# A row pool of its own, down weights behind the rows, and a later last routing in a two-layer mixture-of-experts kernel

## The chip, the cores and the metric

The kernel runs as one program on one core of a Trainium2 chip. The metric is the device time of one execution in microseconds (us). TensorE (PE) does the matrix products and the transposes, VectorE (DVE) and ScalarE (ACT) the elementwise work and the copies out of PSUM, GpSimd (POOL) issues the indirect DMAs (scatters and gathers by a list of row numbers), and SyncE (SP) issues most of the plain DMAs. An engine takes its instructions in order. A DMA issue that has to wait on a semaphore holds back everything queued behind it on the engine that issues it.

## The reference

Eight sequences of 512 tokens with 256 features, in float32, go through two pre-norm layers:

```python
x = x + L0_attn(layernorm(x))   # causal, 16 query heads, 4 key/value heads, rotary
x = x + L0_ffn(layernorm(x))    # 32 experts of inner size 96, top 8 of a softmax, weights renormalized
x = x + L1_attn(layernorm(x))   # causal, 16 heads, biases
x = x + L1_ffn(layernorm(x))    # 16 experts of inner size 176, top 2, and one shared expert of 352
# an expert e: (silu(t @ gate_e) * (t @ up_e)) @ down_e, times the token's routing weight
```

Layernorm is over the features and has no scale or bias.

## The kernel before

**Stages.** The first attention runs sequence by sequence in a software pipeline; after each sequence comes its routing (`routed0`): normalize, turn, router scores, top 8, and then 32 indirect DMAs on POOL (line 427, `xg<-xn_f,rows_f`) that scatter the token rows into a table `xg` in DRAM, ordered by expert. The experts of layer 0 follow, then the second attention with its routing (8 scatters a sequence) and the shared expert, and then the experts of layer 1. The tokens are split into two parts (sequences 0 to 3 and 4 to 7), each with its own tables.

**Experts.** `experts` runs over pairs of tiles of 128 rows: 150 pairs in layer 0 (75 a part), some 44 in layer 1. Step `s` of the loop issues five stages, each for another pair: `load` of pair s (two DMAs from `xg` on SP, line 1141, into a tile `xg_m`, seven of them in rotation), `turn_x` of pair s-4 (PE transposes to `xgT_m`, a DVE copy to `xgTs_m`), `gate_up` of pair s-5 (products `gu_m`, silu on ACT, scaling on DVE to `h_m`), `turn_h` of pair s-6 (`hT_m`, copied to `hTs_m`) and `down` of pair s-7 (products `y_m` with the weights `dw`, line 1214, copied by ACT to `ys_m` and stored). PE's order is that of the loop, written by hand; the other engines are ordered by a scheduler. Row numbers are read into SP registers every eight tiles (line 1119).

After step 3, `load_down` issues the DMAs of the down weights on SP (line 1303): 6 of them, 3.15 MB, in layer 0; 26, 2.88 MB, in layer 1. The list `Beside` steps other work along with the pairs. In layer 0 that is the routing of the last sequence (13 steps over pairs 7 to 20), then the tables and zero rows of the second part (line 1076, `xg<-zeros`), loads of weights, and the gathers `x_a<-yg` that add the experts' results to the first sequences.

**Memory.** Pools are opened one after another and take addresses in that order; a stage's pools reuse the addresses of the stage before. A tile that lies where an older one lay waits for the last reader of the older one. In the kernel before, `xg_m` belongs to the experts' pool `moe` and lies at its bottom, below `xgTs_m`, `h_m`, `hTs_m` and `ys_m`. In the attention, `oT_a` (the turned output, read by the output products `y_a`, line 769) and `xn_f` (the normalized rows that the scatters read) are tiles that matter below.

**Normalization.** `layernorm_steps` computes statistics (lines 315, 316), the inverse root in small steps (281 to 290) and the scaled rows `xn` (325). Its argument `behind` names an instruction after which each operation is put on its engine's queue. `layernorm` runs all of it at once. For the first sequence of the second attention that instruction is the last `hTs_m` copy of the experts, so the whole normalization comes after it; later sequences use the attention's last mask product.

**Startup.** `fast0` loads the attention's weights. The key and value weights pass through one buffer `kv_in`, and the cosine and sine tables through one buffer `turnf`, so the second of each is issued on ACT's queue when the first has been read.

Of the kernel before, what the change touches and what calls it, by code (L numbers as in the profile page):

```python
# [17 lines left out]
P = 128  # L18
# [4 lines left out]
NG = 4  # L23
# [68 lines left out]
def two_blocks_kernel(  # L92
# [212 lines left out]
    def layernorm_steps(x, lnp, name, tag="xn", bufs=1, spare=0, behind=lambda: None):  # L305


        def later():
            return tc.issue_after(behind()) if behind() else ExitStack()

        stats = lnp.tile([P, NT, 6], F32, tag="stats", name=f"stats_{name}")
        mv = lnp.tile([P, NT, 2], F32, tag="mv", name=f"mv_{name}")
        for t in range(NT):
            with later():
                nc.vector.bn_stats(out=stats[:, t, :], in_=x[:, t, :])
            nc.vector.bn_aggr(out=mv[:, t, :], in_=stats[:, t, :])  # L316
            if t % 2:
                yield
        with later():
            rstd = inverse_root(mv[:, :, 1], lnp, name)  # L320
        yield
        xn = lnp.tile([P, NT, D + spare], F32, tag=tag, name=f"xn_{name}", bufs=bufs)
        for t in range(NT):
            with later():
                nc.vector.tensor_scalar(
                    xn[:, t, :D], x[:, t, :], mv[:, t, 0:1], rstd[:, t : t + 1], ALU.subtract, ALU.mult
                )
            if t % 2:
                yield
        return xn  # L330
# [501 lines left out]
    def fast0(awp, lnp, atp, late, ptp, ps, bank):  # L832
# [10 lines left out]
                nc.vector.tensor_copy(q_out[:, :, :, s, :], q_in[:, k, :, s, :, :DH])  # L843
        for n, which in enumerate("kv"):
            lo, hi = A0[which]
            kv_in = awp.tile([P, ND, NG, 32], F32, tag="kv_in", name=f"{which}_in", bufs=1)
            nc.scalar.dma_start(out=kv_in.rearrange("p k g r -> p (k g r)"), in_=a0[:, lo:hi])
            at = D + n * HKV * DH
            nc.vector.tensor_copy(
                wq[:, :, at : at + HKV * DH].rearrange("p k (g d) -> p k g d", g=HKV), kv_in[:, :, :, :DH]  # L850
            )
# [2 lines left out]
        turn = []  # L854
        for which in ("cos", "sin"):
            lo, hi = A0[which]
            f = awp.tile([DH, T], F32, tag="turnf", name=f"{which}f", bufs=1)
            nc.scalar.dma_start(out=f, in_=a0[:DH, lo:hi])
            tr = bank(f"{which}t")[:, : NT * DH].rearrange("p (t d) -> p t d", t=NT)
            for t in range(NT):  # L860
                nc.tensor.transpose(tr[:, t, :], f[:, t * P : (t + 1) * P], ident[:DH, :DH])
            w = awp.tile([P, NT, DH], F32, tag=which, name=f"{which}0")
            nc.vector.tensor_copy(w, tr)
            turn.append(w)
# [98 lines left out]

        return w, loads

    def fast1(w, v1s, lnp, atp, late, ptp, ps, bank, last):
        wv, wo, vb, ob, qkb = (w[n] for n in ("v", "o", "vb", "ob", "qkb"))
        att = Attention(1, late, ptp, ps, bank, wo, last)

        def before(b):  # L970
            x, name = xs[b], f"a1_{b}"
            xn = layernorm(x, lnp, name, behind=att.masked)
            yield from free()
            xn = yield from turned(xn, lnp, bank, name)

            nc.vector.tensor_tensor(
                x, x, ob.rearrange("p m d -> p (m d)").unsqueeze(1).to_broadcast([P, NT, D]), ALU.add
            )
            v1 = v1s[b % 2]
            for h in range(NT // 2):  # L980
                v = bank(f"v_{name}_{h}").rearrange("p (t d) -> p t d", t=2)
                for i in range(2):
                    t = 2 * h + i
                    for k in range(ND):
                        nc.tensor.matmul(
                            v[:, i, :], xn[:, k, t * P : (t + 1) * P], wv[:, k, :], start=(k == 0), stop=(k == ND - 1)
                        )
                for i in range(2):
                    nc.vector.tensor_tensor(
                        v_heads(v1, 2 * h + i, H), v[:, i, :].rearrange("p (h d) -> p h d", d=DH), vb, ALU.add  # L990
                    )
                yield
            qT = atp.tile([P, 2, T], F32, tag="qT", name=f"qT_{name}")
            kT = atp.tile([P, 2, 2, T], F32, tag="kT", name=f"kT_{name}")
            for m in range(2):
                q = bank(f"q_{name}_{m}")
                for k in range(ND):
                    nc.tensor.matmul(q, w["q"][:, k, m, :], xn[:, k, :], start=(k == 0), stop=(k == ND - 1))  # L998
                nc.vector.tensor_scalar(qT[:, m, :], q, qkb[:, 0, m : m + 1], None, ALU.add)
                yield  # L1000
                kk = bank(f"k_{name}_{m}")
                for k in range(ND):
                    nc.tensor.matmul(kk, w["k"][:, k, m, :], xn[:, k, :], start=(k == 0), stop=(k == ND - 1))
                nc.scalar.activation(
                    kT[:, m, 0, :], kk, AF.Identity, bias=kb[:, m, 0:1], scale=half[:, 0:1]
                )
                nc.vector.tensor_scalar(
                    kT[:, m, 1, :], kk, half[:, 1:2], kb[:, m, 1:2], ALU.mult, ALU.add
                )
                yield  # L1010
            att.heads[b] = lambda c: (qT[:, c // 2, :], kT[:, c // 2, c % 2, :], v1, c * NG * (DH + 1))

        return att, before
# [67 lines left out]
    class Beside:  # L1081


        def __init__(self, *items):
            self.items = []
            for item in items:
                self.add(*item)
            self.load = None
            self.last = None

        def add(self, first, last, steps, work):
            self.items.append([first, last, steps, iter(work), 0])
# [10 lines left out]
            for item in self.items:  # L1103
                drain(item[3])

    def experts(n, gu, dn, mp, ps, again, beside, load_last):

        name = f"m{n}{'g' * again}"
        jobs = [(lay, i) for lay in lays[n] for i in range(0, lay.tiles(again), 2)]
# [25 lines left out]
        def load(lay, i):  # L1135
            part = lay.part
            if i % RB == 0:
                registers(lay, i)
            xg = mp.tile([P, 2, lay.width], F32, tag="xg", name=f"xg_{name}_{part}_{i}", bufs=7)
            for j in range(2):  # L1140
                beside.load = nc.sync.dma_start(out=xg[:, j, :], in_=lay.xg[bass.ds(rows[part, i + j], P), :]).ins
            made["xg", part, i] = xg
# [53 lines left out]
        def turn_h(lay, i):  # L1196
            part = lay.part
            h = made.pop(("h", part, i))
            hp = ps.tile([P, n_ch, 2, P], F32, tag="hT", name=f"hT_{name}_{part}_{i}")
            hT = mp.tile([P, n_ch, 2, P], F32, tag="hTs", name=f"hTs_{name}_{part}_{i}")  # L1200
            for q, (lo, n_in) in enumerate(chunks):
                for j in range(2):
                    nc.tensor.transpose(hp[:n_in, q, j, :], h[:, j, lo : lo + n_in], ident)  # L1203
            beside.last = nc.vector.tensor_copy(hT[: chunks[0][1]], hp[: chunks[0][1]]).ins  # L1204
            made["hT", part, i] = hT

        def down(lay, i):
# [78 lines left out]
                in_ = src[n][:, : 2 * ND * P].rearrange("p (g c i) -> p g c i", c=ND, g=2)  # L1286
                nc.sync.dma_start(out=out_[:, g, :, at : at + hi - lo], in_=in_[:, g, :, lo:hi])

    def load_down(w, src, inner, routed):

        chunks = -(-inner // P)
        width = inner // chunks
# [5 lines left out]
        for n, lo, hi, e, at in pieces(inner, whole):  # L1298
            while lo < hi:
                q, r = at // width, at % width  # L1300
                rows = min(hi - lo, width - r)
                to = (e * chunks + q) * D
                nc.sync.dma_start(out=w[r : r + rows, :, to : to + D], in_=src[n, lo : lo + rows, :, 2 * ND * P :])
                lo, at = lo + rows, at + rows

    def read_x(b, tmp, tiles=NT):
# [92 lines left out]
    def all_experts(n, gw, gat, again=False, weights=()):  # L1399
# [6 lines left out]
        with ExitStack() as s:  # L1406
            dwp = s.enter_context(tc.tile_pool(name=f"down{n}{g}", bufs=1, reuse_waits="tile"))
            mp = s.enter_context(tc.tile_pool(name=f"moe{n}{g}", bufs=3, reuse_waits="tile"))
            small = s.enter_context(tc.tile_pool(name=f"tables{n}{g}", bufs=1, reuse_waits="tile"))
            ps = s.enter_context(tc.tile_pool(name=f"ps_m{n}{g}", bufs=2, space=PSUM, reuse_waits="tile"))  # L1410
            inner, chunks, src, routed = (I0, 1, f0, N0) if n == 0 else (I1, ND1, f1, N1R)
# [28 lines left out]
            if n == 0 and not again:  # L1440
                beside.add(8, 9, 1, x_kept())
                lnp = s.enter_context(tc.tile_pool(name="ln_last", bufs=1, reuse_waits="tile"))
                beside.add(7, 20, 13, routed0(NB - 1, lnp, bank, ffn_parts(lnp, bank)[0], lambda: beside.last))
                begin = 22
            beside.add(
                begin, min(32 + begin, first - 4), 6 + lays[n][1].n_e // 8, tables(lays[n][1], small, bank, again, beside)
            )
# [5 lines left out]
            else:  # L1453
                beside.add(
                    done, end, SPLIT[1] * 7, results(range(SPLIT[1]), gat, gat, ps, g, lambda: beside.last)
                )
            experts(n, gw, dw, mp, ps, again, beside, lambda: load_down(dw, src, inner, routed))
            return beside.last

    def routed0(b, lnp, bank, route, behind=None):  # L1460
        name = f"f0_{b}"
# [32 lines left out]
    with ExitStack() as s1:  # L1494
        wp1 = s1.enter_context(tc.tile_pool(name="attn_w1", bufs=1, reuse_waits="tile"))
        gat = s1.enter_context(tc.tile_pool(name="gather", bufs=1, reuse_waits="tile"))
        w1, loads1 = weights1(wp1)
        last = all_experts(0, gw0, gat, weights=loads1)
        with ExitStack() as s:
            awp, lnp, atp, late, ptp, smp, ps = pools(s, 1, False)  # L1500
            v1s = v_tiles(awp, 2, H, nc.vector)
            bank = banks(ps, 3)
            att, before = fast1(w1, v1s, lnp, atp, late, ptp, ps, bank, last)
            route, shared = ffn_parts(smp, bank)
            gw1 = gpool.tile([P, E1 * GU1], F32, tag="gu", name="gw1")

# [280 lines left out]
```

## Time and profile before

| what | value |
|---|---|
| median of 14 runs | 1957.71 us (1945.08 to 1967.18) |
| profiled execution, whole | 1952.44 us |
| its span, first to last instruction | 1950.6 us |
| mean granted PE clock | 0.897 |
| PE busy | 1592.0 us, 82% |
| DVE, ACT, POOL busy | 994.1, 650.4, 811.2 us |
| first attention | to about 640 us |
| experts of layer 0 | about 640 to 1132 us |
| second attention | about 1132 to 1690 us |
| experts of layer 1 and results | about 1690 to 1950 us |

The table is one profiled execution; the other runs have a time only. Busy time overlaps between engines. "Granted clock" is the share of full speed that PE was given.

### The profile page before, as it was taken

The numbers are of one execution on the slowest core, as the hardware profiler recorded it, in microseconds if no ns is written. First come the engines' busy times: TensorE is split into PE (matmuls) and PEld (weight loads), VectorE is DVE, ScalarE is ACT, GpSimd is POOL, SyncE is SP. The second block draws the span as 40 slices with busy tenths as digits, with TensorE's granted clock in tenths as the row PEclk, the third lists the DMA queues.
The fourth block names the chain that finished last, engine by engine and source line by source line (L and its number), as shares of the span: only waits on it lengthen the run. The fifth ranks groups of instructions, "written<-read, shape, count | busy, mean of one in ns | idle before, by whom it ended". The sixth has DMA issues, their size and how long they took to land.

```text
span 1950.6 us, 31020 instructions
## 1 busy us (share of the span) xinstructions
PE 1592.0 (82%) x10180; PEld 1050.0 (54%) x10180; DVE 994.1 (51%) x3179; ACT 650.4 (33%) x865; POOL 811.2 (42%) x686
## 2 busy tenths in 40 slices
PE   5977385575835658999999979999999997999995
PEld 3433142232413657989988844445444544677764
DVE  5655273453623434545555666566546645444453
ACT  3533142232412112323333334454444543222222
POOL 0041623515245151000788888388884011133332
PEclk9977696777867778999999989999999998999997
DMA  2132332522124655787999975256642022435364
GB/s 64 32 104 71 108 88 92 167 86 85 59 84 136 191 173 156 217 258 205 250 262 272 276 142 71 63 97 128 133 72 66 21 84 69 139 102 161 92 215 153
DMA packets 245721, 255.75 MB, mean 131 GB/s; under 512 B 79881, under 2 KB 224911, under 8 KB 245554
## 3 DMA queue, kind: packets, MB, share of 16 engines
q1 hardware_dynamic: 188754, 164.15, 28.1%
q0 software_dynamic: 56448, 89.18, 19.9%
q8 instruction: 88, 1.44, 0.3%
q14 instruction: 79, 0.65, 0.1%
q10 hardware_dynamic: 352, 0.33, 0.1%
HBM read 132.37 MB, written 124.32 MB: 132 GB/s over the span
## 4 chain that ended last, share of the span: by engine, by line
PE 62%; another core or an unknown queue 14%; DVE 9%; issue 6%; ACT 5%; DMA 2%; SPq 1%; POOL 0%; DVEq 0%; POOLq 0%; ACTq 0%
PE gu_m L1183 13%; PE y_m L1214 8%; PE st_a L680 8%; PE o_a L703 6%; PE xgT_m L1150 4%; ACT p_a L685 3%; PE hT_m L1203 2%; PE y_a L769 2%; PE sy_f L457 2%; PE qkv_a L887 2%; PE sg_f L444 2%; PE su_f L444 2%; DVE p_a L691 2%; PE q_a L998 1%
## 5 line engine op out<-in xcount | busy, mean ns | idle before, releaser
L427 POOL DMA_INDIRECT xg<-xn_f,rows_f x320 | 316.5, 989 | 674.3 <-DVE rec_a L719 243.5
L1263 POOL DMA_INDIRECT x_a<-yg,yrows x256 | 402.7, 1573 | 289.1 <-DVE yrows L1260 193.1
L685 ACT ACTIVATE p_a<-st_a 128x2048 f32<-128x2048 f32 (+1 forms) x192 | 306.1, 1594 | 372.9 <-PE st_a L680 230.9
L1183 PE MATMUL gu_m<-gw,xgTs_m 128*128 x1552 | 341.7, 364 | 21.1 <-issue 12.5
L680 PE MATMUL st_a<-qT_a,kT_a 32*128 32x512 f32 (+3 forms) x2048 | 217.3, 499 | 94.9 <-ACT p_a L685 76.7
L1183 PEld LDWEIGHTS gu_m<-gw,xgTs_m 128*128 128x128 f32 x1552 | 262.8, 195 | 51.5 <-issue 14.4
L691 DVE TENSOR_TENSOR p_a<-p_a,causal 128x512 f32<-128x512 f32 x256 | 170.6, 685 | 140.9 <-ACT p_a L685 127.5
L1214 PE MATMUL y_m<-dw,hTs_m 96*128 (+1 forms) x952 | 240.1, 382 | 2.7 <-DVE mv_f L316 2.7
L703 PE MATMUL o_a<-p_a,v 128*32 128x512 f32 (+3 forms) x2048 | 212.3, 476 | 19.7 <-issue 13.4
L680 PEld LDWEIGHTS st_a<-qT_a,kT_a 32*128 32x128 f32 x2048 | 96.3, 196 | 195.1 <-ACT p_a L685 103.7
L1152 DVE COPY xgTs_m<-xgT_m 128x512 f32<-128x512 f32 x194 | 133.5, 688 | 107.1 <-PE xgT_m L1150 68.5
L1219 ACT COPY ys_m<-y_m 128x512 f32<-128x512 f32 x194 | 113.7, 586 | 205.1 <-PE y_m L1214 161.3
L1214 PEld LDWEIGHTS y_m<-dw,hTs_m 96*128 96x128 f32 (+1 forms) x952 | 166.8, 192 | 18.5 <-DVE mv_f L316 2.9
L1175 DVE SCALAR_TENSOR_TENSOR h_m<-h_m,xg_m,gu_m 128x96 f32<-128x96 f32 (+1 forms) x388 | 114.7, 326 | 91.2 <-ACT h_m L1188 39.2
L1225 POOL DMA_INDIRECT yg<-ys_m,to_m x88 | 88.9, 1010 | 154.1 <-ACT ys_m L1219 139.5
L1204 DVE COPY hTs_m<-hT_m 96x256 f32<-96x256 f32 (+1 forms) x194 | 92.8, 478 | 113.9 <-PE hT_m L1203 85.0
L1150 PE MATMUL xgT_m<-ident,xg_m 128*128 128x128 f32 x776 | 121.3, 278 | 30.1 <-DMA xg_m<-xg 15.5
L1191 ACT ACTIVATE h_m<-gu_m 128x192 f32<-128x192 f32 x150 | 49.7, 331 | 253.1 <-PE gu_m L1183 183.8
L1150 PEld LDWEIGHTS xgT_m<-ident,xg_m 128*128 128x128 f32 x776 | 96.6, 143 | 54.7 <-issue 19.7
L709 DVE COPY osb_a<-o_a 128x512 f32<-128x512 f32 x64 | 44.1, 689 | 160.1 <-remote 86.8
L703 PEld LDWEIGHTS o_a<-p_a,v 128*32 128x32 f32 x2048 | 52.1, 113 | 131.7 <-issue 91.0
L1203 PE MATMUL hT_m<-ident,h_m 128*96 128x128 f32 (+1 forms) x476 | 86.1, 277 | 15.3 <-DVE h_m L1175 15.1
(206 smaller groups left out, 1704.2 us busy)
## 6 DMA issues: line engine op xcount, KB each, us to landing
xg_m<-xg SPq DMA_DIRECT2D x388, 144.0 KB
yg<-ys_m SPq DMA_DIRECT2D x150, 256.0 KB
xg<-zeros SPq DMA_DIRECT2D x100, 144.0 KB
g<-yg SPq DMA_DIRECT2D x16, 512.0 KB
xg<-xn_f,rows_f POOLq DMA_INDIRECT x320
x_after<-x_in SPq DMA_DIRECT2D x8, 512.0 KB
x_a<-x_after SPq DMA_DIRECT2D x8, 512.0 KB
x_a<-yg,yrows POOLq DMA_INDIRECT x256
```

The source lines that it names most:

```text
L427: inst = nc.gpsimd.indirect_dma_start(out=lay.xg, out_offset=bass.IndirectOffsetOnAxis(ap=rows[:, t, i : i + 1], axis=0), in_=xn[:, t, :], ...
L680: nc.tensor.matmul(st[:, g, at : at + T - j * P], kT[r, j * P : (j + 1) * P], qT[r, j * P :], start=True, stop=True,)
L685: nc.scalar.activation(pt, st[:, :, :width], AF.Exp, scale=SCALE)
L691: self.masked = nc.vector.tensor_tensor(d, d, causal.unsqueeze(1).to_broadcast([P, NG, P]), ALU.mult).ins
L703: nc.tensor.matmul(o[32 * g : 32 * g + 32, j * P :], v1[:, j, v_at + g * (DH + 1) :][:, :32], probs[n][:, g, at : at + T - j * P], start=( ...
L1150: nc.tensor.transpose(tr[:, j, c, :], xg[:, j, c * P : (c + 1) * P], ident)
L1152: nc.vector.tensor_copy(xT, tr)
L1175: nc.vector.scalar_tensor_tensor(h[:, j, :], h[:, j, :], xg[:, j, D:][:, bass.ds(offs[part, i + j][2], 1)], gus[j][:, inner:], ALU.mult, A ...
L1183: nc.tensor.matmul(gus[j], xT[:, j, c, :], gu[:, bass.ds(at + c * 2 * inner, 2 * inner)], start=(c == 0), stop=(c == ND - 1),)
L1203: nc.tensor.transpose(hp[:n_in, q, j, :], h[:, j, lo : lo + n_in], ident)
L1214: nc.tensor.matmul(y[:, j, :], hT[:n_in, q, j, :], dn[:n_in, bass.ds(at + q * D, D)], start=(q == 0), stop=(q == n_ch - 1),)
L1263: nc.gpsimd.indirect_dma_start(out=xs[b][:, t, :], out_offset=None, in_=lay.yg[: lay.tiles(bool(again)) * P, :], in_offset=bass.IndirectOf ...
```

## The change

1. The row tiles `xg_m` get a pool of their own, `rows`, opened after `moe`, so they lie above the experts' other buffers (in layer 0 at 181,696 bytes of each partition instead of 161,984; in layer 1 at 208,832 instead of 175,552).
2. `load_down` puts its DMAs behind the last row load issued so far (`beside.load`), which is the eighth.
3. The last sequence's routing steps along pairs 20 to 33 instead of 7 to 20, and the second part's tables begin at pair 36 instead of 22.
4. The first normalization of the second attention is spread: its nine groups go behind the last six `hTs_m` copies, the list of which `experts` now keeps, instead of behind the last one.
5. `kv_in` and `turnf` have two buffers each, which moves later attention tiles up by 3,072 bytes.
6. `later` calls `behind` once for each operation instead of twice, as an iterator now needs.

```diff
         def later():
-            return tc.issue_after(behind()) if behind() else ExitStack()
+            inst = behind()
+            return tc.issue_after(inst) if inst else ExitStack()
...
-            kv_in = awp.tile([P, ND, NG, 32], F32, tag="kv_in", name=f"{which}_in", bufs=1)
+            kv_in = awp.tile([P, ND, NG, 32], F32, tag="kv_in", name=f"{which}_in", bufs=2)
...
-            f = awp.tile([DH, T], F32, tag="turnf", name=f"{which}f", bufs=1)
+            f = awp.tile([DH, T], F32, tag="turnf", name=f"{which}f", bufs=2)
...
-    def fast1(w, v1s, lnp, atp, late, ptp, ps, bank, last):
+    def fast1(w, v1s, lnp, atp, late, ptp, ps, bank, copies):
-        att = Attention(1, late, ptp, ps, bank, wo, last)
+        att = Attention(1, late, ptp, ps, bank, wo, copies[-1])
...
-            xn = layernorm(x, lnp, name, behind=att.masked)
+            if b == 0:
+
+                behind = iter([copy for copy in copies[-6:] for _ in range(2)])
+                xn = whole(layernorm_steps(x, lnp, name, behind=lambda: next(behind)))
+            else:
+                xn = layernorm(x, lnp, name, behind=att.masked)
...
-            xg = mp.tile([P, 2, lay.width], F32, tag="xg", name=f"xg_{name}_{part}_{i}", bufs=7)
+            xg = xgp.tile([P, 2, lay.width], F32, tag="xg", name=f"xg_{name}_{part}_{i}")
...
             beside.last = nc.vector.tensor_copy(hT[: chunks[0][1]], hp[: chunks[0][1]]).ins
+            beside.copies.append(beside.last)
...
-    def load_down(w, src, inner, routed):
+    def load_down(w, src, inner, routed, behind):
...
-                nc.sync.dma_start(out=w[r : r + rows, :, to : to + D], in_=src[n, lo : lo + rows, :, 2 * ND * P :])
+                with tc.issue_after(behind):
+                    nc.sync.dma_start(out=w[r : r + rows, :, to : to + D], in_=src[n, lo : lo + rows, :, 2 * ND * P :])
...
             mp = s.enter_context(tc.tile_pool(name=f"moe{n}{g}", bufs=3, reuse_waits="tile"))
+
+            xgp = s.enter_context(tc.tile_pool(name=f"rows{n}{g}", bufs=7, reuse_waits="tile"))
...
-                beside.add(7, 20, 13, routed0(NB - 1, lnp, bank, ffn_parts(lnp, bank)[0], lambda: beside.last))
-                begin = 22
+                beside.add(20, 33, 13, routed0(NB - 1, lnp, bank, ffn_parts(lnp, bank)[0], lambda: beside.last))
+                begin = 36
...
-            experts(n, gw, dw, mp, ps, again, beside, lambda: load_down(dw, src, inner, routed))
-            return beside.last
+            experts(n, gw, dw, mp, xgp, ps, again, beside, lambda: load_down(dw, src, inner, routed, beside.load))
+            return beside.copies
```

More of the change, by code (lines that the diff above doesn't have):

```diff
@@ L1089, in __init__ @@
             self.last = None
+            self.copies = []
         def add(self, first, last, steps, work):
@@ L1104, in finish, with experts @@
                 drain(item[3])
-    def experts(n, gu, dn, mp, ps, again, beside, load_last):
+    def experts(n, gu, dn, mp, xgp, ps, again, beside, load_last):
         name = f"m{n}{'g' * again}"
@@ L1497, in two_blocks_kernel @@
         w1, loads1 = weights1(wp1)
-        last = all_experts(0, gw0, gat, weights=loads1)
+        copies = all_experts(0, gw0, gat, weights=loads1)
         with ExitStack() as s:
@@ L1502, in two_blocks_kernel @@
             bank = banks(ps, 3)
-            att, before = fast1(w1, v1s, lnp, atp, late, ptp, ps, bank, last)
+            att, before = fast1(w1, v1s, lnp, atp, late, ptp, ps, bank, copies)
             route, shared = ffn_parts(smp, bank)
```

## The prediction

> **What bounds it now.** I read the page first, then the chain of waits stage by stage, then the SP queue's own timeline and waits, because most of the change moves DMA issues.
>
> ```profile
> PE 62%; another core or an unknown queue 14%; DVE 9%; issue 6%; ACT 5%; DMA 2%; SPq 1%; POOL 0%; DVEq 0%; POOLq 0%; ACTq 0%
> ```
>
> The chain that ended last lies on TensorE for 62%, so an edit counts where it opens or closes a PE gap. The stretches around the edits (columns: length, busy us of PE, PE weight loads, DVE, ACT, POOL, granted clock, DMA share, GB/s):
>
> ```profile
> 641.00:658.00 17.00, 9.91 (x43) 8.74 (x44) 5.73 (x16) 0.99 (x3) 0.05 (x1) 0.68 0.74 181
> 649.00:653.00 4.00, 4.00 (x20) 3.87 (x20) 1.23 (x4) 0.66 (x2) 0.00 (x0) 0.62 1.06 236
> 658.00:698.00 40.00, 39.13 (x250) 35.94 (x249) 25.50 (x100) 14.75 (x29) 0.13 (x1) 0.96 0.65 196
> 698.00:745.00 47.00, 16.70 (x73) 13.86 (x72) 6.17 (x17) 3.46 (x8) 30.68 (x32) 0.59 0.42 145
> 1645.00:1662.00 17.00, 15.66 (x47) 10.04 (x48) 9.71 (x35) 3.65 (x5) 0.31 (x1) 0.80 0.79 180
> 1701.00:1760.00 59.00, 59.00 (x290) 44.78 (x289) 28.04 (x83) 14.12 (x35) 22.53 (x23) 1.00 0.35 108
> ```
>
> Seen here: once the first down product of a layer has run (658 and 1701), PE has no gap, so a late start is never made up. While the 32 scatters of the last sequence's routing leave POOL (698 to 745), PE works 16.7 of 47 us. The SP queue at both starts of experts:
>
> ```profile
> 606.35 2.45 SPq L1303 DMA_DIRECT2D dw<-in_f_dram  x4
> 610.16 37.18 SPq L1141 DMA_DIRECT2D xg_m<-xg  x8
> 647.38 0.93 SPq L1303 DMA_DIRECT2D dw<-in_f_dram  x2
> ...
> 1645.59 13.34 SPq L1303 DMA_DIRECT2D dw<-in_f_dram  x26
> 1660.05 9.54 SPq L1141 DMA_DIRECT2D xg_m<-xg  x14
> ```
>
> ```profile
> SPq L1141 <- remote: 28.2, 1, 28.2
> ```
>
> In layer 0 four of six down-weight loads leave at 606, under the attention's tail; then two row loads; then the third waits 28.2 us (612.05 to 640.24), until the attention's last output product. In layer 1 all 26 weight loads leave at 1645, 55 us before they are needed. The first down products, by the chain:
>
> ```profile
> 656.57 0.92 issue
> 657.49 1.12 PE y_m L1214 x4
> ...
> 1700.87 1.73 PE y_m L1214 x8
> ```
>
> In layer 0 it starts as the last weight load lands (last semaphore step at 657.4); in layer 1 nothing holds it.
>
> **Part 1: weights behind rows, layer 0: +7 us.** The new row pool lies above the expert buffers, and the two doubled startup buffers push the attention's late tiles up by 3 KB per partition. By the addresses of the built program the first row buffer now overlaps oT of the last sequence; before, the third load's buffer did. So the 28.2 us wait moves from the third load to the first, and all six weight loads stand behind eight row loads, where before four stood ahead of them. First row load at 640.35. The trace has six row loads from there to 647.38 (slow at first, 0.52 us each at the end); two more end at 648.4. Then 6 weight loads of 3.15 MB, where before 2.1 MB of it was in by 617. Rates of the nearest rows: 236 GB/s (649 to 653, mostly these weights) and 181 (641 to 658). From 649.3 that is 13.4 to 17.4 us, landing at 662.7 to 666.7 against 657.4: +5.2 to +9.2. I take +7, nearer neither end. Rows 9 and up are behind the weights and come with them. The first transposes slip some 2 us, hidden under that wait. The cover is gone from here on: PE is full after 658.
>
> The Trainium skill, "DMA: Bandwidth & Descriptors", in its anatomy of one DMA, fits a transfer as 2.0 us plus bytes over 436 GB/s. By that the 3.15 MB would take 9.2 us and this part would cost about +1; for the 2.88 MB of layer 1 it gives 8.6 us and about 0 there. No stretch of several us in which these weights move, in 1 KB packets, is above 240 GB/s, so the rows decide and the sum leaves the fit out.
>
> **Part 2: the same in layer 1: +9.5 us.** Here the first row buffer is free early, but by the built program the second pair's overlaps xn of the last sequence's routing, so the third row load waits for all eight of its scatters. The last one on POOL:
>
> ```profile
> 1685.31 0.96 POOL L427 DMA_INDIRECT xg<-xn_f,rows_f  x1 [0.30 <-issue]
> ```
>
> Its packets end at 1687.9 in the trace. SP goes on at 1688; six row loads at 0.52 us; weights from 1691.1, 26 loads. Before, these took 16.6 us from first issue (1645.6) to last packet (1662.2): so 1707.7, and 0 to 3 us more for the 0.9 MB of rows ahead. At 236 GB/s it would be 1704.5. Taken: 1708.5 against 1700.87, +7.6 (bounds +3.6 to +9.8). The first down product waits for all 26 by its semaphores. The pair's own rows (issued 1688) are in by about 1691, when needed. PE then idles some 7.6 us from a clock of 1.00. After an idle of 9 us it restarted thus:
>
> ```profile
> 743.96 0.67 PE L1203 MATMUL hT_m<-ident,h_m 128*96 128x128 f32 x2 [9.01 <-DVE h_m L1175]
> 744.42 1.92 PE L1214 MATMUL y_m<-dw,hTs_m 96*128 x4
> ```
>
> The same groups take 0.38 and 1.03 us when warm; with the next two (1.06 for 0.60, 1.77 for 1.47) that is 1.9 us lost. +1.9 (0 to 1.9); in layer 0 the trace of before already holds such a restart, so nothing is added there. PE is full to 1860, so all of it reaches the end.
>
> **Part 3: last routing at pairs 20 to 33: 0.** Same 13 steps, same 32 scatters, same table loads, 13 pairs (37 us at 2.83 us a pair) later. The stall of some 30 us in 698 to 745 moves with the scatters. Bounds from the other bursts: over eight stretches of 40 to 42 us PE was busy 13.3 to 19.8 us, so idle 22 to 28 against 30: -8 to +3. The part tables and 33 zero writes move from the loads of pairs 44 to 53 to those of 58 to 67; the rows that need them are first read at pair 75. In 825 to 845, where most of these writes leave, PE lost 2.3 us; that moves too.
>
> **Part 4: first normalization in steps: -2.7.**
>
> ```profile
> 1130.68 1.92 PE L1214 MATMUL y_m<-dw,hTs_m 96*128 x8
> 1135.92 1.69 PE L343 MATMUL xT_a<-ident,xn_a 128*128 128x128 f32 x8 [3.32 <-DVE xn_a L325]
> ```
>
> PE waits 3.32 us for the statistics. In steps they run behind the last six hT copies: 5.4 us of DVE work (4 statistics, 4 aggregates, 12 small operations, 4 scalings) in pairs where DVE has 1.65 us of work in 2.83, so 7.1 us are free. Small delays of the copies give back about 0.6. Bounds -3.3 to +1.
>
> **Part 5: startup: -0.7.**
>
> ```profile
> 4.37 4.66 DMA sinf<-in_a_dram
> ...
> 9.72 0.23 DVE sin L863
> ```
>
> The sine table was issued only when the cosine buffer was free; now at about 2.1. On DVE the query weights' copies end at 9.04, the sine's starts at 9.72: 0.7 us, then bound by the query weights' landing (about 8), a little later as the value weights now go ahead. Bounds -1.4 to 0.
>
> **Sum.** 7 + 9.5 + 0 - 2.7 - 0.7 = +13.1. The profiled execution took 1952.44 us (span 1950.6, 1.8 around it): 1965.5. It ran 5.3 below the median, 1957.71, so the forecast is 1970.8.
>
> **Rivals.** (a) *The loads come faster than the rows say*: both weight loads at 236 GB/s or better, no restart loss. Then +5.2 and +3.6 against -3.4 of gains: +5, and with row waits that end earlier about +2: 1960. For it: the layer 1 loads may have been slowed by the attention around them. Against: both stretches show DMA engines busy at 0.74 or more. 0.14.
> (b) *Faster*: the routing's burst at its new place stops PE less. The eight scatters of 1676 to 1686 left PE busy 13.6 of 14 us, so a burst needn't stop it. If two thirds or more of the 30 us go, the sum falls to -7 or below, 1951 or less; it decides from 19 us saved. Against: all eight bursts of 32 stopped PE alike, in attention and in the experts, and nothing in it is changed but its place. 0.11.
> (c) *Both starts dearer*: stragglers and rows behind the weights cost 4 to 5 us more each: 1980 and above. 0.08.
> (d) *The edit doesn't do what it says*, rows earlier: that is in the forecast, since the addresses undo it in both layers.
> Forecast: 0.67.
>
> **Numbers.** A measurement of this kernel can tell about 0.3%, 5.9 us. The forecast's own terms span +5 to +23; its lower edge touches "same". Slower 0.74, same 0.15, faster 0.11. The range leaves out most of (b) and half of (c): 1956 to 1982.
>
> **What would show it.** After: SP's wait of some 28 us ahead of the first row load at 640, six weight loads at about 648, first down product of layer 0 near 664; SP waiting until 1688 (shifted by the sum so far), the first down product of layer 1 7 to 8 us later than its transposes allow; the 3.32 us before xT_a gone. Wrong if either first down product isn't late, or if PE is busy over 30 us in the 47 us of the moved burst.

## The result and the profile after

The changed kernel takes 1977.96 us (median of 10 runs, 1969.69 to 1987.27), against 1959.4 us for the kernel before (47 runs): ratio 1.0099, 95% interval [1.0071, 1.0128], so 14 to 25 us slower. The forecast was 1970.8 us, with a range of 1956 to 1982. Its profiled execution took 1971.17 us (span 1969.5), 18.7 more than the one of before.

From the page, the shares of the chain that ended last; TensorE still carries it:

```profile
PE 61%; another core or an unknown queue 15%; DVE 8%; issue 5%; ACT 4%; DMA 3%; SPq 2%; POOL 1%; ACTq 0%; DVEq 0%; POOLq 0%
```

The SP queue at the start of layer 0 (start, length, line, operation, count), then its wait in 600 to 760:

```profile
619.51 22.72 SPq L1148 DMA_DIRECT2D xg_m<-xg  x8
642.33 3.64 SPq L1312 DMA_DIRECT2D dw<-in_f_dram  x6
646.77 14.71 SPq L1148 DMA_DIRECT2D xg_m<-xg  x9
```

```profile
SPq L1148 <- remote: 27.8, 1, 27.8
```

The wait that stood ahead of the third row load is now ahead of the first, and all six weight loads stand behind eight row loads. Before, four had left at 606. One detail is new: the wait ended at 619.37, not at 640, and then each of the eight loads took 2.8 us to issue. The same stretch by windows (length, busy us of PE, PE weight loads, DVE, ACT, POOL, granted clock, DMA share, GB/s), with the moved burst of 32 scatters in the last line:

```profile
641.00:664.00 23.00, 10.48 (x37) 9.22 (x38) 4.58 (x12) 2.86 (x5) 0.00 (x0) 0.58 0.90 207
664.00:704.00 40.00, 40.00 (x257) 37.31 (x255) 22.85 (x63) 12.82 (x28) 0.00 (x0) 1.00 0.69 210
...
736.00:783.00 47.00, 16.45 (x79) 13.04 (x77) 6.66 (x21) 3.71 (x9) 30.66 (x32) 0.75 0.44 149
```

Transfers fill the wait (DMA share 0.90), PE is then full, and the burst stops PE as before (16.45 of 47 us busy, against 16.70). The chain at the first down product of layer 0:

```profile
652.37 7.69 DMA xg_m<-xg
660.06 2.03 PE y_m L1222 x4
```

It names a row load, the last transfer to step a semaphore. By the program `y_m` reads `dw`, whose loads left SP just before on the same queue, so the weights are what it waits for; the profile alone doesn't say so. Layer 1, by the chain, the SP queue and PE's timeline:

```profile
1696.10 0.96 POOL xg L428
...
1697.36 2.43 DMA xg<-xn_f,rows_f
...
1699.99 0.33 SPq L1148
```

```profile
1676.75 26.17 SPq L1148 DMA_DIRECT2D xg_m<-xg  x8
1703.04 13.17 SPq L1312 DMA_DIRECT2D dw<-in_f_dram  x26
```

```profile
1706.44 5.06 PE L1190 MATMUL gu_m<-gw,xgTs_m 128*128 x8 [2.69 <-DVE xgTs_m L1159]
...
1720.81 2.57 PE L1222 MATMUL y_m<-dw,hTs_m 88*128 x8 [2.62 <-DMA xg_m<-xg]
```

The first line is the last scatter but one; the last starts at 1697.36 and its transfer ends at 1699.79. Then comes the third row load, then the 26 weight loads, then the first down product: each step waits for the one above it. After its wait the first group of `gu_m` takes 5.06 us where the same group later takes 2.53. At the turn to the second attention the gap of 3.32 us is gone:

```profile
1136.46 1.93 PE L1222 MATMUL y_m<-dw,hTs_m 96*128 x8
1138.22 1.04 PE L344 MATMUL xT_a<-ident,xn_a 128*128 128x128 f32 x8
```

### The stages of all runs

Lengths in us, worked out from starts and ends in the traces. *L0 start*: from the first scatter of the last burst in the first attention to the first down product. *L0 pairs*: from there to the start of the last one of layer 0. *Norm*: from there to the first `v_a`. *Attention 2*: to the last shared-expert product `sy_f`. *L1 start*: to the start of the 17th down product instruction of layer 1 (the first of its third pair), so the slow products after an idle PE are in it.

| profile | L0 start | L0 pairs | norm | attention 2 | L1 start | span |
|---|---|---|---|---|---|---|
| before | 56.9 | 474.7 | 5.9 | 551.4 | 21.2 | 1950.6 |
| after | 63.5 | 478.0 | 1.6 | 562.0 | 31.0 | 1969.5 |
| weights_first | 55.7 | 480.4 | 1.6 | 547.2 | 26.6 | 1947.3 |
| routing_back | 64.0 | 474.4 | 1.6 | 565.4 | 31.2 | 1978.0 |
| norm_startup | 54.4 | 475.4 | 1.6 | 572.0 | 21.2 | 1960.2 |
| pool_order | 54.5 | 473.0 | 8.6 | 566.5 | 32.6 | 1971.5 |
| *second chip:* before_again | 23.6 | 444.6 | 6.4 | 529.0 | 21.2 | 1659.3 |
| after_again | 28.0 | 443.9 | 1.6 | 528.4 | 31.0 | 1665.3 |
| routing_only | 20.3 | 438.4 | 6.1 | 531.4 | 21.2 | 1652.8 |
| spread_last | 23.8 | 437.8 | 1.6 | 529.5 | 21.2 | 1646.5 |
| *third chip:* after_more | 60.8 | 476.8 | 1.6 | 550.2 | 32.9 | 1957.3 |
| norm_startup_2 | 53.7 | 474.0 | 1.6 | 552.4 | 21.2 | 1938.3 |
| best_later | 53.6 | 475.4 | 1.6 | 565.6 | 21.2 | 1949.3 |
| spread_again | 51.4 | 455.3 | 1.6 | 550.5 | 21.2 | 1912.5 |

From before to after: startup -1.75 (first scatter at 113.59 against 115.34), first attention -2.2, L0 start +6.5, L0 pairs +3.2, norm -4.3, attention 2 +10.6, L1 start +9.8, the rest of layer 1 -3.0. That adds up to the +18.9 of the spans. All but attention 2 and two small negatives (first attention, rest of layer 1) belong to an edit: -1.75 + 6.5 + 3.2 - 4.3 + 9.8 = +13.5.

### The profile page after: what moved, and what is told of

It reads as the page before. It is cut to its first block, busy times and chain, and to the rows that moved or that the text cites. A ratio compares the mean times of both kernels' runs of the same rounds, so it can differ in the third digit from the quotient of the medians.

```text
span 1969.5 us, 31022 instructions
## 1 busy us (share of the span) xinstructions
PE 1589.9 (81%) x10180; PEld 1048.7 (53%) x10180; DVE 993.7 (50%) x3179; ACT 649.7 (33%) x865; POOL 808.3 (41%) x686
## 4 chain that ended last, share of the span: by engine, by line
PE 61%; another core or an unknown queue 15%; DVE 8%; issue 5%; ACT 4%; DMA 3%; SPq 2%; POOL 1%; ACTq 0%; DVEq 0%; POOLq 0%
PE gu_m L1190 13%; PE y_m L1222 8%; PE st_a L681 7%; PE o_a L704 6%; PE xgT_m L1157 4%; ACT p_a L686 3%; PE y_a L770 2%; PE hT_m L1210 2%; PE sg_f L445 2%; PE qkv_a L888 2%; PE su_f L445 2%; PE sy_f L458 2%; SPq L1148 2%; DMA xg_m<-xg 2%
## 5 line engine op out<-in xcount | busy, mean ns | idle before, releaser
L1190 PE MATMUL gu_m<-gw,xgTs_m 128*128 x1552 | 344.5, 366 | 29.6 <-DVE xgTs_m L1159 23.8
L704 PE MATMUL o_a<-p_a,v 128*32 128x512 f32 (+3 forms) x2048 | 210.8, 472 | 23.8 <-issue 17.8
L770 PE MATMUL y_a<-wo,oT_a 128*128 128x256 f32 x256 | 74.2, 436 | 28.3 <-issue 19.6
```

Source lines behind the costliest of these rows:

```text
L704: nc.tensor.matmul(o[32 * g : 32 * g + 32, j * P :], v1[:, j, v_at + g * (DH + 1) :][:, :32], probs[n][:, g, at : at + T - j * P], start=( ...
L770: nc.tensor.matmul(y[:, i, :], oT[:, k, t * P : (t + 1) * P], self.wo[:, k, :], start=(k == 0), stop=(k == ND - 1),)
L1190: nc.tensor.matmul(gus[j], xT[:, j, c, :], gu[:, bass.ds(at + c * 2 * inner, 2 * inner)], start=(c == 0), stop=(c == ND - 1),)
```

## Experiments

The theory: the two late expert starts (rows above other buffers, weights behind rows) make the kernel slower, and normalization and startup give a little back. Rivals: the second attention is itself made longer; the place of the last routing matters.

**Weights ahead of the rows again** (the change with item 2 undone):

```diff
-                with tc.issue_after(behind):
-                    nc.sync.dma_start(out=w[r : r + rows, ...
+                nc.sync.dma_start(out=w[r : r + rows, ...
```

> The changed kernel with the down weights no longer put behind the row loads (item 2 undone, the row pool stays on top). Theory (the order costs): in layer 0 four weight loads leave ahead of the blocked row loads again, so the first down product comes some 5 us earlier than in the changed kernel, and in layer 1 all 26 leave about 45 us ahead of the last scatters, so the first down product is at most 2 us late against about 10. In all some 14 us less than the changed kernel, so about 5 us over the kernel before. Rival (the row pool's addresses cost, whatever the order): the row loads still wait for the last output product and for the last scatters, the starts stay late, and the time stays within 4 us of the changed kernel's.

Measured: 1965.51 us (12 runs) against 1962.51 for before (30 runs), ratio 1.0024 [0.9995, 1.0054]. So item 2 carries most of the loss: 12 us by the medians, 15 by the two ratios. Layer 0 starts 1.3 us earlier than before. In layer 1 the expectation missed: the start is still 5.4 us late. SP there, by its timeline:

```profile
1639.52 12.97 SPq L1311 DMA_DIRECT2D dw<-in_f_dram  x26
1658.09 30.47 SPq L1148 DMA_DIRECT2D xg_m<-xg  x14
```

The weights leave early, yet the rows from the third on still wait for the scatters that read `xn_f`, whose place the row buffer overlaps: the last scatter starts at 1678.81, and the third row load leaves at 1681.44. So of the 9.8 us in layer 1 the rows alone make 5.4, and the weights behind them the rest.

**The last routing back at pairs 7 to 20** (the change with item 3 undone):

```diff
-                beside.add(20, 33, 13, routed0(NB - 1, ...
-                begin = 36
+                beside.add(7, 20, 13, routed0(NB - 1, ...
+                begin = 22
```

> The changed kernel with the last routing back at pairs 7 to 20 and the tables from pair 22 (item 3 undone). Theory (the zero rows collide with the turn from part one to part two): the stretch around pairs 67 to 80, where PE loses about 11 us to late rows in the changed kernel, loses about 3 us at pairs 50 to 58 instead, so 7 us less than the changed kernel. Rival (as predicted: the move is worth nothing): within 2 us of the changed kernel in that stretch, both terms only shifted.

Measured: 1975.56 us (7 runs), ratio 1.0074 [1.0043, 1.0106]. The pairs of layer 0 take 474.4 us, as before, against 478.0: 3.6 us belong to the later routing, half of what the theory said. In the changed kernel, PE's waits in 860 to 905 (engine, line, releaser: us in total, times, longest) hold this line, and before had one such wait, of 2.2 us, in 820 to 860:

```profile
PE xgT_m L1157 <- DMA xg_m<-xg: 5.7, 4, 2.2
```

The zero rows of the second part's table share SP's queue with the row loads. Moved 14 pairs later they stand near the turn from one part to the next, where PE waits four times instead of once. Other profiles agree in size: in 800 to 1120 PE's waits for rows make 5.6 to 6.7 us in the three with item 3 as the change has it (after, weights_first, after_more) and 2.2 to 4.0 in before, routing_back, norm_startup, pool_order and norm_startup_2.

**Normalization and startup alone** (before with items 4 to 6):

```diff
-            kv_in = awp.tile(..., bufs=1)
+            kv_in = awp.tile(..., bufs=2)
...
+                behind = iter([copy for copy in copies[-6:] for _ in range(2)])
+                xn = whole(layernorm_steps(x, lnp, name, behind=lambda: next(behind)))
```

> The kernel before with the first normalization in steps and the two startup buffers doubled (items 4 to 6 alone). Theory: -1.7 us at the start, -3 to -4.5 us where the second attention begins, and the second pair's rows of layer 0 no longer wait for the last output product (0 to -3 us at its first down product): 5 to 9 us faster. Rival (DVE work among the last pairs is given back, and the stalls of the first attention swallow the startup's gain): 0 to 2 us faster.

Measured: 1956.96 us (12 runs), ratio 0.9964 [0.9941, 0.9987], 7 us faster than before: norm -4.3, startup -1.2, and -2.5 at the start of layer 0. There SP's longest wait ahead of a row load is 21.1 us instead of 28.2; that the 3,072 bytes do this by freeing the row buffers earlier is argued, not shown. Its profile fell on its slowest run (span 1960.2): attention 2 took 572 us in it.

**Row pool and weights, without the startup buffers** (before with items 1 and 2):

```diff
+            xgp = s.enter_context(tc.tile_pool(name=f"rows{n}{g}", bufs=7, reuse_waits="tile"))
...
+                with tc.issue_after(behind):
+                    nc.sync.dma_start(out=w[r : r + rows, ...
```

> The kernel before with the row pool on top and the weights behind the rows (items 1 and 2 alone, startup buffers single, so the attention's late tiles lie 3 KB lower). Theory (addresses decide): in layer 0 the first row buffer is free early, so eight row loads leave at about 610 and all six weight loads before 640, and the first down product comes 1 to 4 us earlier than before; in layer 1 the third row load still waits for the last scatters, and the first down product is about 10 us late: +6 to +9 us in all. Rival (the order alone decides): layer 0 is some 6 us late too, +16 us in all.

Measured: 1972.49 us (12 runs), ratio 1.0045 [1.002, 1.007], 9 us slower. Layer 1 is late as in the change (32.6 us); layer 0 is not late at all (54.5). By SP's timeline, the eight row loads leave from 597.83 on and the weights behind them:

```profile
597.83 4.09 SPq L1141 DMA_DIRECT2D xg_m<-xg  x8
606.65 4.02 SPq L1304 DMA_DIRECT2D dw<-in_f_dram  x6
611.79 40.70 SPq L1141 DMA_DIRECT2D xg_m<-xg  x9
```

The same queue order costs 6.5 us or nothing in layer 0, depending on which old tile lies under the first row buffer. Two startup buffers, 600 us earlier in the program, decide it: routing_back, which has them, needs 64.0. The gap before the second attention is 2.7 us longer here than before (8.6); in it PE waits a second time, 2.10 us, while DVE fills `v` ahead of the last scaling of `xn`. The expectation didn't have that.

**The pair on a second chip**, both kernels unchanged; a single run each:

> The kernel before, profiled once more. The second attention, from its first value product to the last shared-expert product, took 551 us in the profile of before and 562 in that of the changed kernel, and 547 to 572 in the four experiments, though the order on PE is the same in all. Theory (it varies from execution to execution, by the stalls while POOL gathers and scatters): some other length, anywhere in 545 to 572, for the same kernel. Rival (it belongs to the kernel): 551 to 552 again.

> The changed kernel, profiled once more. Theory: layer 0's start (last scatter burst of the attention to the first down product) 63 to 64 us, layer 1's (last shared product to the first down product) 19 to 20 us, the first normalization's gap 1.6 us, all as in its first profile, since nothing in them is left to chance; the second attention's length is another one than 562. Rival (the starts vary too, and the first profile was a draw): either start 3 us or more away from its first value.

Measured: 1661.07 and 1667.09 us (median of before there 1658.15, 23 runs). This chip runs the same program 300 us faster. The late starts are there too: L0 start +4.4, L1 start +9.8, norm -4.8, while attention 2 differs by 0.6 us. As expected of the changed kernel, layer 1's first down product comes 19.3 us after the last shared one and the normalization's gap is 1.6; layer 0's start does not (28.0 us instead of 63 to 64), and attention 2 of before (529.0) lies outside both guesses: they were made for a chip like the first. What the chip lacks is the stall; the last burst of 32 scatters on it, by windows:

```profile
467.34:507.54 40.20, 39.45 (x252) 36.02 (x251) 22.66 (x65) 12.51 (x27) 30.75 (x32) 1.00 0.93 301
```

POOL is as busy as on the first chip (30.75 us), but PE works 39.45 of 40.2 us at full clock.

**The later routing alone, on the second chip** (before with item 3; the diff is routing_back's, reversed):

> The kernel before with the last routing at pairs 20 to 33 and the tables from pair 36 (item 3 alone). Theory (zero rows meet the turn of the parts): from the first to the last down product of layer 0 it takes 478 to 481 us instead of 474.7, with PE waiting for rows two or more times at pairs 73 to 80; 3 to 6 us slower in all. Rival (as predicted): 474 to 476 us and no difference in time.

Measured: 1653.88 us (12 runs), ratio 0.9969 [0.9951, 0.9988], 5 us faster. Both expectations missed. The pairs of layer 0 take 438.4 us against 444.6. In before_again PE lost the following while the last routing stepped at pairs 7 to 20 (PE's waits, 430 to 450), and this kernel has no such wait. DVE's timeline names its cause:

```profile
PE gu_m L1183 <- DVE xgTs_m L1152: 5.7, 1, 5.7
```

```profile
438.23 0.73 DVE L325 TENSOR_SCALAR xn_f<-x_in,mv_f,rstd_f 128x256 f32<-128x256 f32 x2 [6.91 <-DMA xg<-xn_f,rows_f]
```

The last routing's `xn_f` waits for the scatters of the sequence before, and DVE's copies for PE stand behind it. That burst runs from 396.2 to 436.4 there, beyond the first down product (419.8). In before on the first chip it is over at about 641, ahead of the first down product at 657.5, so there was no such wait to save. Nor does the later place always save it: in after_again, which has item 3 too, the pairs take 443.9 us, and in spread_last below, whose routing also begins at pair 7, they take 437.8 without that wait.

**The last routing's scatters spread out** (norm_startup, with the 32 scatters in four groups of 8, six pairs apart):

```diff
-                beside.add(7, 20, 13, routed0(NB - 1, ...
+                routing = routed0(NB - 1, ...)
+                beside.add(7, 20, 13, islice(routing, 12))
+                beside.add(20, 38, 3, routing)
...
+                for t in range(NT):
+                    for i in range(k):
+                        inst = nc.gpsimd.indirect_dma_start(out=lay.xg, ...)
+                    yield
```

> Items 4 to 6 on the kernel before, and the 32 scatters of the last sequence's routing (layer 0) in four groups of eight, each group's row numbers made six pairs (17 us) after those of the group before. Theory (PE stops because a long unbroken run of scatters builds up a lag of the semaphores, and eight at a time do not): from the first to the last down product 447 to 456 us instead of 475, some 25 us less than the same kernel without the groups, about 30 us faster than before. Rival (each scatter costs PE its share, however they are spread): 473 to 477 us, no more than the 7 us that items 4 to 6 gave.

Measured: 1650.6 us (12 runs), ratio 0.9952 [0.9934, 0.9971]. The stall it should remove does not exist on this chip, so it says nothing of the burst's length, and the expectation's 447 to 456 us don't apply (437.8). It was run again on a third chip, where before takes 1940.62 us (19 runs), with three others.

**The change once more, on the third chip:**

> The change as it stands, beside the three below on one chip. Theory (late starts of both expert stages, +6.5 and +9.8, zero rows +3, less 6 for normalization and startup): 10 to 16 us slower than before on a chip where before takes about 1960, and 6 to 11 slower where before takes about 1660. Rival (the second attention itself is made some 10 us longer by the change): 19 or more slower where before takes 1960, and the stretch from the first v_a to the last shared product over 560 us again.

Measured: 1958.59 us (4 runs), ratio 1.0108 [1.0047, 1.0168]. The median is 18 us above before's, past the theory's 10 to 16, but the interval reaches from 9 to 33 and cannot decide by itself. The stage does: attention 2 took 550.2 us, 12 less than in the first profile of the same program, and on one chip it is no longer than in norm_startup_2 below (552.4), which has neither late start: the rival falls. Where the two profiles part, by windows from the third and the fourth group of 8 scatters on; first the slower profile:

```profile
1399.00:1419.00 20.00, 10.19 (x80) 4.38 (x80) 9.47 (x33) 5.96 (x6) 16.00 (x14) 0.74 0.80 205
1469.00:1489.00 20.00, 15.40 (x136) 7.37 (x135) 11.37 (x36) 8.83 (x7) 8.04 (x8) 0.91 0.29 93
```

and the later run of the same program:

```profile
1397.00:1417.00 20.00, 15.70 (x118) 8.82 (x116) 15.15 (x50) 9.06 (x8) 16.34 (x13) 0.91 0.76 184
1470.00:1490.00 20.00, 19.07 (x143) 11.30 (x142) 16.50 (x55) 10.14 (x10) 8.59 (x9) 1.00 0.22 67
```

PE loses 5.5 and 3.7 us more in one run than in the other, in stretches that the change doesn't touch.

**The yardstick on the third chip** (norm_startup again):

> Before plus the normalization in steps and the two doubled startup buffers, the yardstick for the two below. Theory: 5 to 9 us faster than before on either chip (normalization 4.3, startup 1 to 2, second pair's rows 1 to 3). Rival (the gain of the first run was chance): within 3 us of before.

Measured: 1934.11 us (10 runs), ratio 0.9952 [0.9921, 0.9984], 9 us faster (3 to 15). Attention 2 took 552.4 us where the profile of the same program on the first chip took 572.0. The change stands 24.5 us above this kernel by medians; its L0 start (+7.1), L0 pairs (+2.8) and L1 start (+11.7) make 21.6 of that.

**The later routing with its zero rows earlier** (norm_startup plus item 3, tables at pairs 34 to 56):

```diff
-                begin = 22
+                begin = 34
...
-                begin, min(32 + begin, first - 4), ...
+                begin, min((22 if begin > 30 else 32) + begin, first - 4), ...
```

> Norm_startup plus the last routing at pairs 20 to 33, with the second part's tables and zero rows at pairs 34 to 56 instead of 36 to 68, so that none of their writes stands near the turn from one part to the next (pair 75). Theory 'the later routing is free, its zero rows at the turn cost 3': first to last down product of layer 0 as in norm_startup within 2 us where before takes 1960, and 4 to 6 shorter where before takes 1660; total equal to norm_startup there, or 5 below it. Rival (the place of the routing itself costs): the stretch 3 us or more longer than in norm_startup.

Measured: 1938.98 us (10 runs), ratio 0.9985 [0.9955, 1.0015]. The pairs of layer 0 take 475.4 us, 1.4 more than in norm_startup_2 and inside the 2 us expected. The median is 4.9 above that kernel's, with overlapping intervals; its profile drew an attention 2 of 565.6. PE still waits 4.3 us for rows in 760 to 900, against 3.9 in norm_startup_2 and 5.8 in after_more. So the later place of the routing by itself costs little, and no gain over norm_startup is shown.

**The spread scatters on the third chip:**

> Norm_startup plus the last routing's 32 scatters in four groups of 8, six pairs apart. Theory 'the stall of PE comes from the length of the burst' (bursts of 8 outside gathers leave PE busy): where before takes 1960, first to last down product 15 to 28 us shorter than in norm_startup, total 15 to 28 below it; where before takes 1660, 4 to 6 shorter, as no stall is there. Rival 'each scatter stops PE by its own share, however grouped': the stretch within 4 us of norm_startup's where before takes 1960.

Measured: 1916.85 us (4 runs, 1906.58 to 1922.44), ratio 0.9876 [0.9811, 0.994]: 24 us faster than before, and 17.3 below norm_startup_2 by medians. The stretch is 455.3 us against 474.0, 18.7 shorter. The burst of 32 in norm_startup_2, by windows:

```profile
687.30:727.47 40.17, 14.42 (x69) 11.95 (x67) 4.54 (x12) 2.42 (x5) 30.71 (x32) 0.67 0.49 165
```

and the four groups of 8 in this kernel:

```profile
685.86:695.68 9.82, 8.45 (x52) 7.40 (x50) 3.07 (x8) 1.62 (x4) 7.68 (x8) 1.00 0.81 261
711.11:720.92 9.81, 7.22 (x46) 6.36 (x44) 3.51 (x11) 1.25 (x3) 7.67 (x8) 1.00 0.66 219
732.00:741.83 9.83, 7.62 (x49) 6.93 (x48) 3.24 (x10) 1.48 (x4) 7.70 (x8) 1.00 0.71 229
755.10:764.91 9.81, 8.93 (x56) 7.87 (x54) 4.45 (x14) 1.25 (x3) 7.67 (x8) 1.00 0.67 221
```

POOL's work is the same (30.7 us in all), but PE goes from 14.42 of 40.17 us busy to 32.22 of 39.27. Idle time falls from 25.8 us beside one run of 32 to 7.1 beside four runs of 8, so the stall grows faster than the number of scatters in an unbroken run; the rival "each scatter has its own price" falls. The later place alone doesn't do it: in best_later and in the change the moved burst of 32 leaves PE busy 0.37 and 0.32 of its 40 us. This version beats both kernels where the stall exists.

## Why the prediction was right, step by step

**Part 1, layer 0 (+7): +6.5, by two errors that cancel.** The wait moved to the first row load, and rows and weights stood in the order foretold. But the wait ended at 619.37, not 640. The prediction read 640 as the end of the last output product, and that reading fails: in before the last `y_a` instruction starts at 618.8, and the addition that reads the products follows 21 us later, 0.11 us ahead of the row load. After the change the last `y_a` starts at 610.5, and the same addition comes 9 us later, again just ahead of the row load. Both lines lie in a burst of scatters:

```profile
640.24 0.69 DVE L773 TENSOR_TENSOR x_in<-x_in,y_a 128x512 f32<-128x512 f32 x1 [11.94 <-remote]
...
619.42 0.69 DVE L774 TENSOR_TENSOR x_in<-x_in,y_a 128x512 f32<-128x512 f32 x1 [5.01 <-remote]
```

So a late release set that time, not the product, and how late it comes differs from profile to profile (21 and 9 us). The loads then crept out, mostly under the scatter burst (596.6 to 637.0), so that the weights left at 642.3. In that kernel's own time, which is 4.0 us earlier at that point (its last burst starts at 596.6, before's at 600.6), the prediction had them leave at 645.3. They then took 17.7 us to the first down product, where 15.2 was taken. That 3.0 us early and 2.5 us long nearly cancel is luck. The trade-off on the fit in the Trainium skill, "DMA: Bandwidth & Descriptors" (anatomy of one DMA), ends on the side of the rows: it gives 9.2 us for these 3.15 MB, and the trace shows 207 GB/s, rows and weights together, with the DMA engines 0.90 busy. That section gives its fit for DMAs issued by GpSimd, and these are issued on SP; so the rows show that the fit doesn't carry over to them, and no run here tests it on its own ground. pool_order shows the condition: with other addresses this part costs nothing.

**Part 2, layer 1 (+9.5): +9.8,** and +11.7, +11.4, +10.0 and +9.8 in after_more, pool_order, routing_back and after_again. Of the 9.8, 8.0 are lateness (7.6 foretold) and 1.75 slow products after the idle: from the first down product to the 17th it takes 11.70 us against 9.95 (1.9 foretold). From the start of the last scatter to the first down product it took 23.45 us (1697.36 to 1720.81); the prediction's times give 1708.5 - 1685.3 = 23.2. One thing was not seen: the prediction had the pair's own rows in "when needed", but PE waits for the rows as well, and weights_first shows 5.4 us of lateness from that alone. The weights hide it in the sum.

**Part 3, routing (0): +3.2.** The mis-sized term. The burst was indeed only moved (16.45 of 47 us busy). The sentence "that moves too" on the zero writes was wrong: they cost 5.7 us of PE waits at their new place against 2.2, and routing_back returns 3.6 us of the stage. The 5 us that this edit alone gains on the second chip are not the lower bound of -8 come true: that bound stood for a burst that stops PE less, and the gain comes from a wait on the burst before.

**Part 4, normalization (-2.7): -4.3.** Mis-sized, and below its bound of -3.3: the estimate took only the 3.32 us wait less some delay. From the start of the last down product to the first `v_a` the trace has 5.86 us before, and 1.59 after and in every profile with this edit; the eight transposes behind the wait also fell from 1.69 to 1.04 us.

**Part 5, startup (-0.7): -1.75** by the profile, -1.2 in norm_startup; just past its bound. After the change the query weights' landing bounds it (issued 2.65, landed 8.1), as foretold.

**The sum.** The fixed terms make +13.5 against +13.1. The two large ones were right; the misses of parts 3, 4 and 5 (+3.2, -1.6 and -1.05) cancel by luck. The span of +5 to +23 that the prediction gives for its terms is not what its own bounds add up to, which is -4 to +25. The median moved by 18.6; the interval starts at 14. The rest is not settled in full: attention 2 differs by 12 and by 20 us between two profiles of one program, on different chips, and the 47 runs of before spread over 25 us. So a single profile's +10.6 there can't be read as a cost of the change, but whether the medians hold a few us more of it is open. Rival (b), a burst that stops PE less, did not come from moving the burst; spread_again shows that cutting it up does bring it. Rival (a) fell with the rates of part 1, (c) with both starts within 0.5 us of their terms, and (d) was right to count as part of the forecast: the rows leave later, not earlier.

## What to carry to other kernels

Before moving a pool, look up which old tiles lie under its first buffers: their last readers are the new waits, and everything queued behind that first load on the same engine is late with it. Keep weights that have no reason to wait ahead of loads that do. Where indirect DMAs leave in a long unbroken run and the compute engine thins out beside it, cut the run into short groups with work between them; in this kernel that was worth 17.3 us by the medians on the third chip, where normalization and startup together gave 6.5. Where the burst stops nothing, as on the second chip, there is nothing of this to gain.

## What was not expected of the hardware

The same program has medians of 1959.4 and 1962.5 us in the first comparisons, 1940.6 on the third chip and 1658.2 on the second, where PE is busy for 93% of the span. Most of the difference lies where the bursts of 32 scatters are: from the first burst to the last one of the first attention it takes 485 us on the first chip and 280 on the second, 205 of the 291 us between the spans. PE is busy 0.28 to 0.48 of their 40 us on the two slow chips and 0.98 of the last one on the fast chip, though POOL issues them at the same 1.27 us pitch. During a burst SP's own steps come 0.70 us apart (635.6 to 641.9 in the changed kernel), and work that is ready starts late, as the additions 21 and 9 us behind their products in part 1; groups of 8 leave PE at 0.74 to 0.91 in the experts.

The Trainium skill, "SBUF — State Buffer" (Who interferes with whom), holds that a DMA never contends with a compute engine, and that a DMA which seems stalled by a DVE operation is one of GpSimd's, short of time to write descriptors. The rows here show another case: POOL keeps its pitch, DVE is busy 4.54 of 40.17 us, and it is PE, SP and DVE that stand still. What delays them, and why one chip is free of it, no run here shows.
